# A graph network's node layer: inputs fetched at the batch's own step, three result buffers, the own rows' part computed early; remainders of A and B by a product with minus identity

## The chip, the cores and the metric

The kernel runs on one core of a Trainium2 chip. The metric is device time in microseconds (us), the median over runs of the whole program; lower is better. PE is the matrix engine, DVE the vector engine, ACT the engine for functions and copies, POOL the general-purpose engine that also issues the indirect transfers, SP the engine that issues most other transfers. "Clock" is the share of PE's full clock that was granted in a stretch of time.

## The reference

One layer of a graph network on 12500 nodes with 64 features and 212500 edges (each of 100000 pairs in both directions, and 12500 loops), sorted by destination; the hidden width is 128. All is float32.

```python
h = jnp.maximum(_layernorm(x, axis=-1), 0.0)
edge_in = jnp.concatenate([h[row], h[col], dist], axis=1)   # row = src, col = dst, dist = edge weight
e = jax.nn.silu(edge_in @ eW1 + eb1)
e = jax.nn.silu(e @ eW2 + eb2)
agg = jax.ops.segment_sum(e, row, num_segments=h.shape[0])
node_in = jnp.concatenate([h, agg], axis=1)
out = x + jax.nn.silu(node_in @ nW1 + nb1) @ nW2 + nb2
```

## The kernel before

**Tiles.** The nodes are in NB = 100 buckets of L = 125, and four buckets (G) make a batch: 25 batches. The first edge layer is split by its inputs, A = h @ eW1[:64] for the source and B = h @ eW1[64:128] for the destination, both made once per node. PE's fast format (fp32r, which `halves` marks) holds fewer bits than float32, so each table row stores a value as its fp32r part and the remainder, and later products add the two. The tables `ta` (A) and `tb` (B) are in DRAM; `tb00` and `tb0` hold B's first 512 and 2048 rows, for the first blocks of edges.

**First stage, A and B.** `normed` normalizes 12 buckets of x at a time. `products` (L751) then takes one batch of four: `turned` (L717) transposes four buckets on PE into `ht` (L721) and ACT copies them to `hr` (L725); `product` (L238) multiplies by eW1's half, two PSUM tiles `ab` with two matmuls each (L246); ACT rounds them to fp32r (L250); after a `yield`, DVE subtracts that part from PSUM to leave the remainder (L253). It does so for A, stores `hr` into the DRAM tensor `hd` (L759) and the rows into `ta`, then for B and `tb`. `first_rows` (L728) does the same for B's first rows. `turns(todo, 3)` runs up to three such generators in turn, and each `yield` is a place where other work is put between.

**Sends.** The edges lie in 208 blocks of 1024. For a block, `count` ranks its edges within their buckets (one-hot comparisons on DVE, running counts through PE into the PSUM tile `misc`, L439 and L463), and `send` fetches B's rows by a selection product on PE (`qp`, L493), copies them to `qs` on ACT (L505, L508; eight buffers), and POOL scatters them by indirect transfers, 128 edges each (L515), to the DRAM queue `q`, at bucket and rank. `send_all` walks over the blocks in pieces: half a block of the send beside a step of the next block's count. During the first 8 blocks and then up to the first level's mark (L905 to L923), two to four yields of the first stage are taken per piece. `counted` (L461) also checks the running counts against the limits that the layout assumes and collects violations in `bad`.

**Levels and batches.** A bucket's queue is read in 14 LEVELS of one or two tiles of 128 edges for each bucket; each level goes through all 25 batches. A batch's `qt` (edges out of `q`, `fetch`, L566, four buffers, so four batches ahead) and `a` (rows of A, `fetch_a`, L581, three ahead) come by SP. A step treats four tiles: `s_one` (L644, one-hot of the place in the bucket, compared with `spots` in PSUM), `s_turn` (its transpose `lr`, L601), `s_pt` (L609: transposed `qt` plus A's rows, then Silu on ACT), `s_bias` and `s_p2` (second layer, L661), `s_seg` (L675, the sum per node into the PSUM tile `seg`), `s_add` (L686, into `aggT` in SBUF). `turn` (L693) lists these in the order in which they are written for successive steps, with `None` where pieces of sends, of the first stage, or of the node layer go in.

**Node layer.** In the last level each batch, once its sums are complete, gets `nodes` (L305). PE forms `z` in two PSUM tiles, the sums' part `w1g` (L312) and the own rows' part `w1n` (L315), 250 columns each; ACT applies Silu; a second product gives `o` (L321); DVE adds x (plus the bias) to `os` (L324); SP sends `os` to the output (L326). Its inputs come through `nodes_in` (L296): `xr`, two loads by SP (L126) and the bias added by POOL, and `hrn`, the load of `hd`. `nodes_in` is called in `fetch` (L579), so four batches ahead, with six buffers (pool `nd_in`); results have two (pool `nd`).

**Order.** The order of PE, DVE, ACT and SP is the order in which the program writes the instructions (`manual_schedule`, L340). How many pieces of sends are put at each `None` follows from fixed marks and planned times (`marks`, L931; `PLAN_...`, L64). PSUM has four rotating buffers for `ab`, `ht`, `qp`, `lr`, `pt`, `z` and `o` (pool `mm`), two for `p2`, one each for `misc` and `seg`. At the very end DVE and PE reduce `bad` to a flag (L976 to L984), which is loaded (L985) and, if it is set, starts a general path (L986) that the given inputs do not take.

Of the kernel before, what the change touches and what calls it, by code (L numbers as in the profile page):

```python
# [28 lines left out]
F32 = mybir.dt.float32  # L29
# [10 lines left out]
P = 128  # L40
# [39 lines left out]
def tile_gnn(ctx: ExitStack, tc: tile.TileContext, x, src, dst, ew, eW1, eb1, eW2, eb2, nW1, nb1, nW2, nb2, out):  # L80
# [112 lines left out]
    nodes_i = const.tile([P, L], I32, name="nodes_i")  # L193
# [3 lines left out]
    diff = const.tile([P, P], I32, name="diff")  # L197
# [3 lines left out]
    for a in range(2):  # L201
        half = slice(a * D, (a + 1) * D)
        nc.gpsimd.dma_start(w1[half, :, :], eW1[: 2 * D, :].rearrange("(s k) f -> k s f", s=2))
    same = const.tile([P, 1], F32, name="same")
# [32 lines left out]

    def product(s, hr, ps, tag, to):  # L238

        abs_ = []  # L240
        for a in range(2):

            half = slice(a * D, (a + 1) * D)
            ab = ps.tile([P, G // 2, H], F32, name="ab", tag=tag)
            for i in range(G // 2):
                nc.tensor.matmul(ab[:, i], hr[half, i, :], w1[half, s, :], start=True, stop=True)  # L246
            abs_.append(ab)
# [3 lines left out]
        yield  # L251
        for a in range(2):
            nc.vector.tensor_tensor(to[:, a, 1], abs_[a], to[:, a, 0], op=OP.subtract)  # L253

    hd = dram.tile([P, NB // 2, P], F32, name="hd")
# [40 lines left out]
    def nodes_in(B, sb):  # L296
# [4 lines left out]
        hr = sb.tile([P, G // 2, P], F32, name="hrn")  # L301
        nc.sync.dma_start(hr, hd[:, b // 2 : b // 2 + G // 2, :])
        return xr, hr

    def nodes(B, xr, hr, ps, sb, tag):  # L305

        b = B * G

        zs = sb.tile([P, 2, G // 2, L], F32, name="zs")
        z = [ps.tile([P, G // 2, L], F32, name="z", tag=tag) for _ in range(2)]  # L310
        for a in range(2):
            nc.tensor.matmul(z[a], w1g, aggT[:, b + a : b + G : 2, :], start=True, stop=False)  # L312
        for a in range(2):
            half = slice(a * D, (a + 1) * D)
            nc.tensor.matmul(z[a], w1n[half, :], hr[half, :, :L], start=False, stop=True)  # L315
        for a in range(2):
            nc.scalar.activation(zs[:, a], z[a], AF.Silu, bias=nb1c)
        yield
        o = ps.tile([L, G, D], F32, name="o", tag=tag)
        for t in range(G):  # L320
            nc.tensor.matmul(o[:, t, :], zs[:, t % 2, t // 2, :], w2n, start=True, stop=True)  # L321
        yield
        os_ = sb.tile([L, G, D], F32, name="os")
        nc.vector.tensor_tensor(os_, o, xr, op=OP.add)  # L324
        yield
# [9 lines left out]
    with ExitStack() as work:  # L335
# [8 lines left out]
        misc = sgp.tile([P, 2 * NB + L], F32, name="misc")  # L344
        upto, numbers, spots = misc[:, :NB], misc[:, NB : 2 * NB], misc[:, 2 * NB :]
        nc.tensor.matmul(upto, before, none, start=True, stop=True)
# [131 lines left out]

        def send(s):
# [56 lines left out]
        def send_all(s0, s1):  # L536

            for s in range(s0, s1):
# [19 lines left out]
        batch, st = {}, {}  # L558
# [3 lines left out]
        def fetch(i):  # L562
# [15 lines left out]
            if c == len(LEVELS) - 1:  # L578
                node_in[B] = nodes_in(B, ndp[0])  # L579
# [29 lines left out]
        def s_pt(k):  # L609
# [23 lines left out]
            c, B, n, g = steps[k]  # L633
            if g == n - 1:
                fetch(c * (NB // G) + B + NQ)
                fetch_a(c * (NB // G) + B + NA)

        def s_one(k):
# [7 lines left out]
                spots[:, None, None, :].to_broadcast(wide),  # L646
# [30 lines left out]
        def s_add(k):  # L677
# [9 lines left out]
            if c == len(LEVELS) - 1:  # L687
                tails.append(nodes(B, *node_in.pop(B), mm, ndp[1], "mm"))
# [39 lines left out]
        def first_rows(g):  # L728
# [4 lines left out]
            yield from product(1, hr, mm, "mm", got)  # L733
# [17 lines left out]
        def products(b0, g, xs):  # L751
# [12 lines left out]
            yield from product(1, hr, mm, "mm", got)  # L764
# [355 lines left out]
```

## Time and profile before

| | before |
|---|---|
| median of 3 runs | 2370.76 us (2369.83 to 2371.57) |
| the profiled execution's own time | 2367.31 us |
| its span in the profile | 2365.5 us |
| mean granted clock | 0.892 |
| PE busy | 2028.7 us, 86% |
| DVE busy | 1814.7 us, 77% |
| ACT busy | 1333.0 us, 56% |
| POOL busy | 1655.9 us, 70% |
| moved by DMA | 572.83 MB, mean 242 GB/s |

The profile is of one execution. The page cuts the span into 40 slices of 59 us with a digit for the busy share of each engine in tenths. Rows that begin with a line number group all instructions of that line, engine and operation: count, busy time, mean ns of one, then the idle time of the engine just before them and what ended most of it. Timelines give start and duration in us and, in brackets, the idle time before an instruction and its releaser. PEld is PE's loading of weights, which overlaps its matmuls. POOL's gap of 0.30 between two scatters is not counted as busy, so its 70% is its share without those gaps.

### The profile page before, as it was taken

Reading aid. Unit: us, or ns where it says so; the run is one execution under the profiler, and the core shown is the slowest. Engines: PE = TensorE matmul, PEld = TensorE weight load, DVE = VectorE, ACT = ScalarE, POOL = GpSimd, SP = SyncE. Lnnn points to the kernel's source line nnn. Section 1 sums busy time; section 2 is a strip of 40 time slices with the busy share of each in tenths; the row PEclk is TensorE's granted clock in tenths of the full one; section 3 lists DMA queues with packets and bytes.
Section 4 is the critical chain, followed back from the end, with each engine's and each line's share of the span. In section 5 each row is a group of like instructions: output and inputs, shape, how many; then the busy total and the mean of one; then the engine's idle time right before and its main releaser. Section 6 shows DMA issues by size and latency. Waiting matters only on the chain.

```text
span 2365.5 us, 47589 instructions
## 1 busy us (share of the span) xinstructions
PE 2028.7 (86%) x16818; PEld 1902.7 (80%) x16818; DVE 1814.7 (77%) x2865; ACT 1333.0 (56%) x2966; POOL 1655.9 (70%) x1724
## 2 busy tenths in 40 slices
PE   4667798952599779969995999999999999989997
PEld 2455697942499669959995999999999999989885
DVE  8899788885488868886886888888888888875221
ACT  3334464631277547737773777666666666656542
POOL 5777777777777777777777777777777777776110
PEclk9655597965699879979996999999999999999998
DMA  5566797964488647867884888888888888878662
GB/s 161 188 235 231 268 298 248 324 225 133 155 297 263 224 170 250 264 197 255 288 286 143 284 280 265 268 276 271 285 267 291 274 275 277 272 244 277 196 196 85
DMA packets 239835, 572.83 MB, mean 242 GB/s; under 512 B 46756, under 2 KB 99072, under 8 KB 239177
## 3 DMA queue, kind: packets, MB, share of 16 engines
q1 hardware_dynamic: 155283, 390.76, 51.5%
q0 software_dynamic: 54112, 124.65, 14.4%
q10 hardware_dynamic: 30196, 54.31, 7.3%
q8 instruction: 136, 2.23, 0.4%
q14 instruction: 108, 0.88, 0.1%
HBM read 356.61 MB, written 212.87 MB: 241 GB/s over the span
## 4 chain that ended last, share of the span: by engine, by line
PE 58%; DMA 12%; DVE 11%; POOL 6%; issue 4%; ACT 2%; SPq 2%; POOLq 0%; DVEq 0%; ACTq 0%
PE seg L675 15%; PE p L661 14%; PE pt L622 10%; DMA q<-qs,to 8%; PE pt L615 6%; POOL q L515 6%; PE qp L493 6%; PE lr L601 4%; DMA out_dram<-os 3%; DVE each L434 1%; DVE oh L426 1%; PE bc L379 1%; DVE rank L453 1%; DVE terms L451 1%; DVE pick L415 1%
## 5 line engine op out<-in xcount | busy, mean ns | idle before, releaser
L515 POOL DMA_INDIRECT q<-qs,to x1661 | 1616.1, 973 | 526.5 <-issue 396.9
L631 ACT ACTIVATE e<-pt 128x512 f32<-128x512 f32 x450 | 268.7, 597 | 496.2 <-PE pt L622 495.2
L675 PE MATMUL seg<-one,e 128*128 128x125 f32 x3600 | 502.3, 283 | 2.0 <-DVE aggT L686 1.7
L661 PE MATMUL p<-w,e 128*128 128x128 f32 x3600 | 498.6, 282 | 0.0
L661 PEld LDWEIGHTS p<-w,e 128*128 128x128 f32 x3600 | 449.9, 195 | 9.9 <-issue 9.2
L675 PEld LDWEIGHTS seg<-one,e 128*128 128x128 f32 x3600 | 444.2, 193 | 9.4 <-issue 4.9
L622 PE MATMUL pt<-oneT,a 125*128 125x128 f32 (+1 forms) x2800 | 423.0, 289 | 14.4 <-DMA a<-ta 8.5
L493 PEld LDWEIGHTS qp<-win,pick 128*128 128x128 f32 x1664 | 268.5, 224 | 202.6 <-ACT qs L505 121.6
L493 PE MATMUL qp<-win,pick 128*128 128x256 f32 x1664 | 347.7, 340 | 93.5 <-ACT qs L505 60.6
L505 ACT COPY qs<-qp 128x512 f32<-128x512 f32 x418 | 245.1, 587 | 323.9 <-DMA q<-qs,to 222.9
L622 PEld LDWEIGHTS pt<-oneT,a 125*128 125x128 f32 x2800 | 356.8, 194 | 18.3 <-issue 9.7
L644 DVE TENSOR_TENSOR one<-misc,qt 128x500 f32<-128x500 f32 x450 | 302.4, 672 | 78.1 <-PE seg L675 42.1
L686 DVE TENSOR_TENSOR aggT<-aggT,seg 128x500 f32<-128x500 f32 x325 | 218.4, 672 | 185.9 <-PE seg L675 182.2
L434 DVE TENSOR_REDUCE each<-oh 128x100 bf16<-128x800 bf16 x208 | 321.0, 1543 | 7.2
L615 PE MATMUL pt<-ident,qt 128*128 128x128 f32 x1800 | 276.3, 277 | 10.4 <-ACT qs L505 10.1
L606 ACT CAST oneT<-lr 125x512 fp32r<-125x512 f32 x450 | 265.5, 590 | 13.2 <-PE lr L601 13.2
L665 ACT ACTIVATE e<-p 128x512 f32<-128x512 f32 x450 | 268.7, 597 | 6.1 <-PE p L661 6.1
L655 ACT COPY p<-b2f 128x512 f32<-128x512 f32 x450 | 267.2, 594 | 0.0
L451 DVE TENSOR_TENSOR terms<-oh,misc 128x800 f32<-128x800 bf16 x208 | 203.6, 979 | 38.2 <-PE misc L439 38.2
L615 PEld LDWEIGHTS pt<-ident,qt 128*128 128x128 f32 x1800 | 215.3, 144 | 19.7 <-ACT qs L505 11.0
L453 DVE TENSOR_REDUCE rank<-terms 128x8 f32<-128x864 f32 x208 | 219.0, 1053 | 7.2
L426 DVE TENSOR_TENSOR oh<-misc,bkt 128x800 bf16<-128x800 f32 (+1 forms) x209 | 203.8, 975 | 2.4 <-ACT bkt L831 2.4
(153 smaller groups left out, 1653.4 us busy)
## 6 DMA issues: line engine op xcount, KB each, us to landing
a<-ta SPq DMA_DIRECT2D x350, 512.0 KB
qt<-q SPq DMA_DIRECT2D x250, 288.0 KB
qt<-q SPq DMA_DIRECT2D x100, 576.0 KB
q<-zeros ACTq DMA_DIRECT2D x25, 1080.0 KB
q<-qs,to POOLq DMA_INDIRECT x1661
win<-tb SPq DMA_DIRECT2D x208, 120.0 KB
tb<-got SPq DMA_DIRECT2D x30, 512.0 KB
q<-zeros ACTq DMA_DIRECT2D x20, 720.0 KB
```

What stands on the lines that cost most here:

```text
L434: nc.vector.tensor_reduce(each, oh.rearrange("p t b -> p b t"), AX.X, OP.add)
L493: nc.tensor.matmul(qp[:, t % 2, :k], halves(pick[:, t * P : (t + 1) * P]), halves(win[:, :k, v]), start=v == 0, stop=v == 1,)
L515: ins = nc.gpsimd.indirect_dma_start(out=q[:], out_offset=bass.IndirectOffsetOnAxis(ap=to[:k, j : j + 1], axis=0), in_=qs[:k, t % 2, a, :] ...
L606: nc.scalar.copy(halves(oneT), st[k].pop("lr"))
L615: nc.tensor.matmul(pt[:, t, :], qt[:, j, :H], ident, is_transpose=True, start=t == 0, stop=False, skip_group_check=True)
L622: nc.tensor.matmul(pt[:, cols, :], halves(a[:L, b, i * H : (i + 1) * H]), halves(oneT[:, cols, :]), start=False, stop=i == 1, skip_group_c ...
L631: nc.scalar.activation(e1, pt, AF.Silu)
L644: nc.vector.tensor_tensor(one.rearrange("p (b j) l -> p b j l", j=n), spots[:, None, None, :].to_broadcast(wide), loc[:, tiles[0][1] : til ...
L655: nc.scalar.copy(p2, b2f)
L661: nc.tensor.matmul(p2[:, t, :], e1[:, t, :], w2, start=False, stop=t == G - 1, skip_group_check=True)
L665: nc.scalar.activation(e2, p2, AF.Silu)
L675: nc.tensor.matmul(item[2][:, b, :], e2[:, t, :], one[:, t, :], start=j < G, stop=j >= G * (n - 1))
```

## The change

- `product` does not yield any more. After ACT's two copies of the fp32r part, PE multiplies that part by `less` (minus identity, made once by DVE) and adds the result into the same PSUM tiles, which then hold the remainder; ACT copies that, where DVE subtracted.
- `products` computes the own rows' part of the node layer, `w1n` times `hr`, for its batch: two matmuls, two ACT copies into `zos`, and a store into the DRAM tensor `own` (250 KB for a batch; it replaces `hd` with 128 KB).
- `nodes` starts from that sum: DVE copies the batch's `zo` into PSUM (`bank`, which lies in `misc`), one matmul over all 500 columns adds the sums' part, and one ACT Silu follows. The copy for the next batch is written behind the `os` of this one. Since `misc` is overwritten, the last level's `s_one` compares with `nodes1` in SBUF.
- `nodes_in` is called in `s_pt` of the batch's own step; the pool of inputs has five buffers instead of six, that of results three instead of two.
- The last level's `fetch` calls are held back until three batches before that level, and then catch up; the last mark of the sends moves with them.
- The last turns of the loop have an order of their own (`ending`).
- The flag is made right behind the last `counted`, in the midst of the last level, by `flagged`; the call that loads it is still written behind the loop, while in the order of the built program SP has the load right behind `flagged`.

```diff
+    less = const.tile([P, P], F32, name="less")
+    nc.vector.tensor_scalar(halves(less), ident, -1.0, None, op0=OP.mult)
...
-                nc.tensor.matmul(ab[:, i], hr[half, i, :], w1[half, s, :], start=True, stop=True)
+                nc.tensor.matmul(
+                    ab[:, i], hr[half, i, :], w1[half, s, :], start=i == 0, stop=False, skip_group_check=True
+                )
...
             nc.scalar.copy(halves(to[:, a, 0]), abs_[a])
-        yield
         for a in range(2):
-            nc.vector.tensor_tensor(to[:, a, 1], abs_[a], to[:, a, 0], op=OP.subtract)
-
-    hd = dram.tile([P, NB // 2, P], F32, name="hd")
+            nc.tensor.matmul(
+                abs_[a], halves(less), halves(to[:, a, 0]), start=False, stop=True, skip_group_check=True
+            )
+        for a in range(2):
+            nc.scalar.copy(halves(to[:, a, 1]), abs_[a])
+
+    own = dram.tile([P, NB // G, G * L], F32, name="own")
...
-        hr = sb.tile([P, G // 2, P], F32, name="hrn")
-        nc.sync.dma_start(hr, hd[:, b // 2 : b // 2 + G // 2, :])
-        return xr, hr
-
-    def nodes(B, xr, hr, ps, sb, tag):
+        zo = sb.tile([P, G * L], F32, name="zo")
+        nc.sync.dma_start(zo, own[:, B, :])
+        return xr, zo
+
+    def nodes(B, xr, zo, ps, sb, tag, bank=None, then=()):
...
+        if bank is not None:
+            nc.tensor.matmul(bank, w1g, sums, start=False, stop=True, skip_group_check=True)
+            nc.scalar.activation(zsv, bank, AF.Silu, bias=nb1c)
...
         nc.vector.tensor_tensor(os_, o, xr, op=OP.add)
+        for more in then:
+            nc.vector.tensor_copy(bank, more())
...
+        bank = misc[:, : G * L]
...
+        def flagged():
+
+            s = wk.tile([P, 1], F32, name="s")
+            nc.vector.tensor_tensor(s, bad[:, 0:1], bad[:, 1:2], op=OP.add)
+            turned_ = mm.tile([1, P], F32, name="turned", tag="mm")
+            nc.tensor.transpose(turned_, s, ident)
+            m = wk.tile([1, 1], F32, name="m")
+            nc.vector.tensor_reduce(m, turned_, AX.X, OP.max)
+            nc.vector.tensor_copy(flag_i, m)
...
                         counted(s)
+                        flagged()
...
+            if c == len(LEVELS) - 1:
+                node_in[B] = nodes_in(B, ndp[0])
             if g == n - 1:
-                fetch(c * (NB // G) + B + NQ)
+                i = c * (NB // G) + B
+                while len(fetched) <= i + NQ and (len(fetched) < final or i + 3 >= final):
+                    fetched.append(0)
+                    fetch(len(fetched) - 1)
                 fetch_a(c * (NB // G) + B + NA)
...
-            yield from product(0, hr, mm, "mm", rows_a)
-            nc.sync.dma_start(hd[:, b // 2 : (b + G) // 2, :], hr)
-            yield
+            product(0, hr, mm, "mm", rows_a)
+            zos = fp1.tile([P, G * L], F32, name=f"zos{b // G % 2}")
+            zo = [mm.tile([P, G // 2, L], F32, name="zo", tag="mm") for _ in range(2)]
+            for a in range(2):
+                half = slice(a * D, (a + 1) * D)
+                nc.tensor.matmul(zo[a], w1n[half, :], hr[half, :, :L], start=True, stop=True)
+            for a in range(2):
+                nc.scalar.copy(zos.rearrange("p (i a l) -> p i a l", a=2, l=L)[:, :, a], zo[a])
+            yield
+            nc.sync.dma_start(own[:, b // G, :], zos)
...
-            start = w * (NB // G) - NQ
+            start = w * (NB // G) - (NQ if w < len(LEVELS) - 1 else 3)
...
+        ending = [(s_add, -2), (s_seg, -1), None, None, (s_add, -1), None, None]
+        for k in range(first, len(steps) + 1):
+            for s in turn if k < len(steps) else ending:
...
-                            for name, bufs in (("nd_in", NQ + 2), ("nd", 2)):
+                            for name, bufs in (("nd_in", NQ + 1), ("nd", 3)):
```

More of the change, by code (lines that the diff above doesn't have):

```diff
@@ L343, in tile_gnn @@
         )
[L344 to L346 removed]
+        misc = sgp.tile([P, G * P], F32, name="misc")
+        upto, numbers, spots = misc[:, :NB], misc[:, NB : 2 * NB], misc[:, 2 * NB : 2 * NB + L]
+        bank = misc[:, : G * L]
+        nc.tensor.matmul(misc, before, none[:, 0:1].to_broadcast([P, G * P]), start=True, stop=True)
         nc.vector.tensor_scalar(numbers, nodes1[:, :NB], -1.0, None, op0=OP.add)
@@ L732, in first_rows @@
             got = fp.tile([P, G, 2, H], F32, name="got", tag="rows")
-            yield from product(1, hr, mm, "mm", got)
+            product(1, hr, mm, "mm", got)
             yield
@@ L763, in products @@
             got = fp.tile([P, G, 2, H], F32, name="got", tag="rows")
-            yield from product(1, hr, mm, "mm", got)
+            product(1, hr, mm, "mm", got)
             yield
@@ L941, in tile_gnn @@
         at = 0
-        for k in range(first, len(steps) + 2):
-            for s in turn:
+        ending = [(s_add, -2), (s_seg, -1), None, None, (s_add, -1), None, None]
+        for k in range(first, len(steps) + 1):
+            for s in turn if k < len(steps) else ending:
                 if s is None:
```

48 lines of the change are left out of this document (21 added, 27 removed).

## The prediction

> **What bounds the kernel now.** I read the page's slices first, then stretches of the span, then POOL's timeline, the chain of waits, and PE and ACT instruction by instruction where the change acts. From the page:
>
> ```profile
> POOL 5777777777777777777777777777777777776110
> PEclk9655597965699879979996999999999999999998
> L515 POOL DMA_INDIRECT q<-qs,to x1661 | 1616.1, 973 | 526.5 <-issue 396.9
> ```
>
> POOL's scatter is equally busy in every slice, though PE's share and clock swing. Four stretches (time; then busy us and count for PE, PEld, DVE, ACT, POOL; granted clock, DMA share, GB/s):
>
> ```profile
> 59.00:177.00 118.00, 77.57 (x354) 58.19 (x355) 106.95 (x188) 44.02 (x126) 85.14 (x85) 0.57 0.60 212
> 1600.00:1800.00 200.00, 197.32 (x1823) 194.00 (x1822) 176.43 (x271) 132.62 (x291) 152.13 (x158) 1.00 0.86 277
> 2093.00:2200.00 107.00, 107.00 (x986) 106.16 (x986) 65.22 (x109) 67.80 (x143) 66.22 (x70) 0.98 0.89 293
> 2200.00:2353.00 153.00, 144.57 (x1121) 123.46 (x1119) 37.17 (x71) 68.88 (x138) 13.98 (x20) 1.00 0.53 158
> ```
>
> 158 scatters in 200 us are 1.27 us each, and 1661 of them are 2110 us: POOL is the bound up to its last scatter. Its timeline shows where it wasn't fed (in brackets the idle time before; 0.30 is normal):
>
> ```profile
> 42.16 1.91 POOL L515 DMA_INDIRECT q<-qs,to  x1 [10.50 <-ACT qs L508]
> ...
> 68.18 0.97 POOL L515 DMA_INDIRECT q<-qs,to  x1 [1.79 <-ACT qs L508]
> 92.30 0.96 POOL L515 DMA_INDIRECT q<-qs,to  x1 [2.98 <-ACT qs L508]
> ...
> 126.13 0.96 POOL L515 DMA_INDIRECT q<-qs,to  x1 [2.73 <-ACT got L250]
> ...
> 2173.32 0.97 POOL L515 DMA_INDIRECT q<-qs,to  x1 [0.30 <-issue]
> ```
>
> These three gaps lose 1.5 + 2.7 + 2.4 = 6.6 us over normal. So the span has three parts: while A and B are made, whatever starves POOL is paid in full, because POOL never idles again; then POOL paces; from about 2093 PE is busy all of 107 us, and after 2200 the node layer rides on each batch. There the chain of waits goes round this loop (start, us):
>
> ```profile
> 2306.90 0.43 DVE os L324
> 2307.35 0.32 SPq L126
> ...
> 2309.09 0.43 SPq L126
> 2309.56 3.47 DMA out_dram<-os
> 2313.16 0.43 DVE os L324
> ```
>
> The sum `os` of one batch frees the buffer for a later `xr`; SP loads that and more, only then sends an older result, and the next `os` waits until that has landed, since results have two buffers: 6.26 us a turn. Without that wait a turn is 5.90 us of PE, from one `z` to the next, 0.62 of it the two own-row products of L315:
>
> ```profile
> 2200.85 0.90 PE z L312 x4
> 2201.75 0.62 PE z L315 x4
> ...
> 2206.75 0.90 PE z L312 x4
> ...
> 2333.60 0.90 PE z L312 x4
> ...
> 2353.00 0.44 DVE os L324
> ...
> 2354.27 0.14 DVE flag_i L984
> ```
>
> **Node layer, part by part.** The inputs of a batch are now loaded in its own step, with five buffers that are free by then, and a result has three: both links of the loop are gone. L315 leaves the step; one product over 500 columns replaces two over 250, at the same 0.90 by column count. PE's turn becomes 5.90 - 0.62 = 5.28. What could hold it above that: DVE gains a copy of 128x500 into the bank, between `os` and the sum into `aggT`. By order, `o` ends 1.19 before the turn's end (0.24 and 0.95 for `lr` and `seg`), `os` takes 0.43 and the copy about 0.67 (the page's 128x500 tensor operations), so it ends with `seg`; the sum into `aggT` follows, 0.67, and `z` is due 1.28 after the turn's start: some 0.4 us to spare. Traffic: 288 KB of `qt`, 512 of `a`, 125 each of `xr` and result, 250 of the saved sum (128 before) are 1300 KB in 5.28 us, 246 GB/s, less than the 293 of the third stretch. On SP the three loads now stand ahead of the turn's `qt` and `a` loads, which have two turns of lead. For 21 turns, from the first `z` to the one at 2333.60: 132.75 before, 21 x 5.28 = 110.9 after, **-21.9**. Bounds: if copy or transfers hold the turn at 5.90, -8.9; nothing goes under 5.28.
>
> From 2333.60 to the end of `os` are 19.8 us. After, by order: `z` and what follows 3.73, then 0.85 for the sum into `aggT`, then 13.2 for the chain through `seg`, `z`, `o` and `os` of the last three batches, one turn fewer but with the last bank copy behind `os`: 17.8, **-2.0** (0 to -3). The flag made after the last `os` ends at 2354.41, 0.97 later than `os`: **-0.9** (0 to -2).
>
> **The flag's new place** costs PE. These rows are PE and DVE around the last count:
>
> ```profile
> 2146.18 0.22 PE L463 MATMUL misc<-each,since 128*128 128x100 bf16 x1
> 2146.43 0.25 DVE L472 TENSOR_TENSOR u<-misc,zone 1x100 f32<-1x100 f32 x1 [1.24 <-PE misc L463]
> 2148.17 0.25 DVE L477 SCALAR_TENSOR_TENSOR misc<-zone,misc 128x100 f32<-128x100 f32 x1
> ```
>
> The new transpose stands right behind L463 on PE and waits for all of DVE's checks and the sum `s`, until about 2148.6; `p2` and the steps behind it wait too, in the stretch where PE has no idle time: **+2.5** (0.2 to 3.5). SP's load of the flag waits for the same, and the `qt` load behind it has two turns.
>
> **A and B: where the sign is decided.** DVE loses 108 subtractions, PE gains 108 products with minus identity and 50 for own rows, ACT 158 copies. A product has no pause in it now, so the 25 groups fall into fewer sends: by order, 50 products, 25 transposes and 25 own-row pairs in 29 half blocks (four scatters, 5.1 us of POOL each, 147 in all), where they filled some 40. The rows, PE and ACT at half clock:
>
> ```profile
> 47.60 1.23 PE L246 MATMUL ab<-w,hr 64*128 64x128 f32 x8 [0.46 <-ACT hr L725]
> 48.76 1.22 PE L493 MATMUL qp<-win,pick 128*128 128x256 f32 x4
> 49.97 0.65 PE L721 MATMUL ht<-ident,x 128*128 128x128 f32 x2
> ```
>
> ```profile
> 47.17 0.37 ACT L725 COPY hr<-ht 128x256 f32<-128x256 f32 x1 [0.34 <-PE ht L721]
> 48.85 0.65 ACT L250 CAST got<-ab 128x256 fp32r<-128x256 f32 x2 [1.31 <-PE ab L246]
> ```
>
> ```profile
> 111.24 1.01 PE L493 MATMUL qp<-win,pick 128*128 128x256 f32 x3 [3.99 <-DVE rows_a L253]
> ```
>
> The last row speaks for the change: PE stood 4 us because a subtraction held a PSUM buffer behind other DVE work. Against it: the minus products wait for ACT's first copies, and all behind them on PE waits too, the next send's `qp` first. A product takes PE 1.23, then a 0.45 gap (copy 0.37, handover 0.08), then two minus products at `qp`'s 0.305: 2.29. The own-row pair is twice L315's 0.62, 1.24. A group: 2 x 2.29 + 1.24 + 0.65 = 6.47, and 0.46 for `hr`; the sends' `qp`, lists and counts some 1.77 a half block. Together 25 x 6.93 + 29 x 1.77 = 225 us at half clock, against POOL's 147; at full clock, with the gaps unshrunk, 25 x (2 x 1.38 + 0.62 + 0.33 + 0.46) + 29 x 0.89 = 130. So each us that PE stays at half clock costs POOL 1 - 147/225 = 0.35 us, and none at full clock. ACT's 135 us fit into 147; DVE, 91% busy in the first stretch, has room now. The scatters' loss of 6.6 goes; the first comes about 1.2 later, as two more products and copies stand before the edge weights' split on ACT. The term is 0.35 t - 5.4, t being the time at half clock: -5.4 to +73. When does the clock rise?
>
> ```profile
> 165.61:169.02 3.41, 3.41 (x21) 2.90 (x19) 2.09 (x4) 0.88 (x3) 2.50 (x4) 0.53 0.52 184
> 169.02:172.43 3.41, 0.13 (x1) 0.00 (x0) 2.97 (x5) 0.30 (x1) 2.80 (x3) 0.97 0.68 237
> 186.09:189.50 3.41, 3.41 (x17) 2.72 (x17) 2.83 (x7) 1.48 (x5) 2.80 (x3) 0.50 1.00 365
> 486.46:489.87 3.41, 2.37 (x22) 2.15 (x20) 3.34 (x4) 2.75 (x8) 2.73 (x3) 1.00 0.93 293
> 489.87:493.29 3.42, 1.61 (x10) 1.26 (x10) 3.32 (x7) 1.62 (x5) 2.51 (x4) 0.97 1.01 346
> 493.29:496.70 3.41, 0.59 (x3) 0.24 (x2) 3.36 (x5) 0.00 (x0) 2.50 (x3) 0.50 1.00 338
> ```
>
> A window of 3.4 us full of PE work raised it once and once not; 69% busy kept it, 47% lost it. In the new stage PE is some 85% busy at half clock, and gap-free runs of 4.8 us (minus products, own rows, a send, the next product: 0.61 + 1.24 + 1.22 + 0.5 + 1.23) come about ten times in the 225 us, every 22; with every second one raising the clock, the first success falls near 45 us. At full clock the stage is some 74% busy, enough to keep it. I take t = 45, nearer the lower end: **+10.3** (0.35 x 45 - 5.4).
>
> The Trainium skill, "TensorE: Matmul & The Clock Gate", section "A second HAM failure mode: psum-queue depth-cycling", tells of a PE that pauses briefly between groups while cycling through PSUM banks and whose clock then swings between half and full; by it t would be some half of the stage, and the time that of the first rival below.
>
> **Sum.** -21.9 - 2.0 - 0.9 + 2.5 + 10.3 = -12.0. The profiled execution took 2367.31 (span 2365.5); the median of the runs is 2370.76, 3.45 more, which I keep: **2359 us**. Larger saved sums (3 MB more to write) hide under a DMA share of 0.60.
>
> **Rivals.** First, slower: PE keeps half clock through the products, its waits for ACT breaking each window. Above t = 78 all gain is gone (0.35 t - 5.4 = 22.3), above 91 it can be told as slower; at half the stage, t = 113, the term is 34 and the time 2383; throughout, 2421. For it: PE never held full clock in 59 to 177 (0.57 granted). Against: there PE waited for DVE, which it won't. Second, the change doesn't do in the last level what it says: the bank copy or a load takes the place of the wait and the turn stays at 5.90, 13.0 more: 2372. For it: one bank, and only 0.4 us to spare. Third, POOL is never starved and the term is -5.4: 2343.
>
> **Chances.** Forecast 0.47, first rival 0.30, second 0.13, third 0.10. What this measurement can tell from no change is about 0.2%, 4.7 us. Faster: forecast and third, less 0.02 at the forecast's edge, 0.55. Within: that 0.02, 0.10 of the second and 0.02 of the first, 0.14. Slower: 0.31. The forecast's own range is t from 15 to 70, 2348 to 2367. The range reaches down into the third and up into the first as far as t = 165: 2344 to 2401.
>
> **What would show it.** Last level: `z` to `z` 5.28, no wait of `os` for the result's transfer; wrong if `z` waits for a DVE copy. Flag: one PE wait of 2.5 us near the last count. A and B: granted clock 1.0 in most of the stretch from 100 to 200, PE waiting for ACT some 0.45 at each minus product, last scatter near 2184. A last scatter after 2196 makes the kernel no faster, and then the forecast is wrong in its choice of t.

## The result, and the profile after

The changed kernel is slower: 2394.11 us (median of 5 runs, 2384.1 to 2401.01) against 2370.76 us (5 runs, 2366.01 to 2371.62); the ratio is 1.0102, 95% interval 1.0084 to 1.0120. The whole interval lies above 1, so it is clear of noise, though small. 2359 had been forecast, with a range that ended at 2401 and a chance of 0.31 for slower. From the page of the profile after:

```profile
span 2392.3 us, 47745 instructions
POOL 5556577777777777777777777777777777777210
PEclk9995588895579969996999899999999999999999
L539 POOL DMA_INDIRECT q<-qs,to x1661 | 1615.4, 973 | 580.7 <-issue 392.7
```

POOL's scatter (now L539) takes as long as before, but stood idle before its instructions for 580.7 us, not 526.5, and its row has fives in the first slices where it had sevens: the 54 us are all at the start. Two of the stretches shown before (time; then busy us and count for PE, PEld, DVE, ACT, POOL; granted clock, DMA share, GB/s):

```profile
59.00:177.00 118.00, 94.92 (x427) 72.14 (x430) 72.14 (x114) 64.73 (x194) 63.70 (x64) 1.00 0.59 210
2200.00:2353.00 153.00, 150.45 (x1283) 140.31 (x1283) 65.53 (x118) 86.06 (x159) 37.09 (x44) 1.00 0.82 263
```

In the first, 64 scatters ran where 85 had. DVE has room now (72 us, 107 before), PE does more (95 us, 78 before). POOL's timeline, its longest gaps between 100 and 250, and its last scatter:

```profile
105.23 0.97 POOL L539 DMA_INDIRECT q<-qs,to  x1 [4.82 <-ACT qs L532]
148.58 0.97 POOL L539 DMA_INDIRECT q<-qs,to  x1 [7.99 <-ACT qs L532]
165.18 0.97 POOL L539 DMA_INDIRECT q<-qs,to  x1 [6.71 <-ACT qs L532]
217.32 0.96 POOL L539 DMA_INDIRECT q<-qs,to  x1 [5.58 <-ACT qs L532]
248.21 0.96 POOL L539 DMA_INDIRECT q<-qs,to  x1 [7.41 <-ACT qs L532]
...
2227.56 0.97 POOL L539 DMA_INDIRECT q<-qs,to  x1 [0.30 <-issue]
```

Below, "starving" is the sum over all scatters of the idle time above the normal 0.30, where a gap is longer than 0.5; some 10 us of it is the wait before the first scatter in every kernel. It is 20.0 us before and 74.5 after, and after 300 us there is none. PE's timeline in the last level (the one product of 500 columns is L322) and around the flag's transpose (L498), and DVE's last `os`:

```profile
2203.58 0.27 PE L498 MATMUL turned<-ident,s 128*1 128x128 f32 x1 [2.47 <-DVE s L496]
...
2258.32 1.10 PE L322 MATMUL misc<-aggT,w1g 128*128 128x500 f32 x2
2263.59 1.05 PE L322 MATMUL misc<-aggT,w1g 128*128 128x500 f32 x2
2268.79 1.05 PE L322 MATMUL misc<-aggT,w1g 128*128 128x500 f32 x2
...
2367.70 1.05 PE L322 MATMUL misc<-aggT,w1g 128*128 128x500 f32 x2
```

```profile
2386.02 0.42 DVE L335 TENSOR_TENSOR os<-o,xr 125x256 f32<-125x256 f32 x1 [3.96 <-issue]
```

With the rows of before that stand in the prediction, the two spans divide at the same events. (These rows of before are from the chain of waits, which starts a `z` 0.16 us later than the timeline does; the second and the fourth row are off by that.)

| stretch | before | after | difference | forecast |
|---|---|---|---|---|
| start to the end of the last scatter | 2174.29 | 2228.53 | +54.2 | +10.3 |
| to the first `z` | 26.56 | 29.79 | +3.2 | +2.5 |
| 21 turns to the 22nd `z` | 132.75 | 109.38 | -23.4 | -21.9 |
| to the end of the last `os` | 19.84 | 18.74 | -1.1 | -2.0 |
| to the end of the span | 12.06 | 5.86 | -6.2 | -0.9 |
| span | 2365.5 | 2392.3 | +26.8 | -12.0 |

So the last level gave what was forecast and more, and the first stage took twice that away.

Of the 18 runs below, 14 fell into times when the kernel before itself took 3500 to 3570 us on the same chip ("disturbed" below); of these, times and ratios are not used, only their last level, whose turn is the undisturbed one (5.21 us for the same code), and once a comparison among themselves.

### The profile page after: what moved, and what is told of

Same layout as the page of the kernel before. It is cut to its first block, busy times and chain, and to the rows that moved or that the text cites. A ratio compares the mean times of both kernels' runs of the same rounds, so it can differ in the third digit from the quotient of the medians.

```text
span 2392.3 us, 47745 instructions
## 1 busy us (share of the span) xinstructions
PE 2060.3 (86%) x16827; PEld 1928.7 (81%) x16876; DVE 1797.1 (75%) x2783; ACT 1379.2 (58%) x3099; POOL 1655.7 (69%) x1724
## 3 DMA queue, kind: packets, MB, share of 16 engines
q8 instruction: 136, 2.23, 0.4%
## 5 line engine op out<-in xcount | busy, mean ns | idle before, releaser
L539 POOL DMA_INDIRECT q<-qs,to x1661 | 1615.4, 973 | 580.7 <-issue 392.7
L690 PEld LDWEIGHTS p<-w,e 128*128 128x128 f32 x3600 | 454.0, 196 | 13.1 <-issue 12.3
L673 DVE TENSOR_TENSOR one<-misc,qt 128x500 f32<-128x500 f32 x425 | 285.9, 673 | 78.8 <-PE seg L704 44.1
L630 ACT CAST oneT<-lr 125x512 fp32r<-125x512 f32 x450 | 265.6, 590 | 12.5 <-PE lr L625 12.5
```

What stands on the lines that cost most here:

```text
L539: ins = nc.gpsimd.indirect_dma_start(out=q[:], out_offset=bass.IndirectOffsetOnAxis(ap=to[:k, j : j + 1], axis=0), in_=qs[:k, t % 2, a, :] ...
L630: nc.scalar.copy(halves(oneT), st[k].pop("lr"))
L673: nc.vector.tensor_tensor(one.rearrange("p (b j) l -> p b j l", j=n), (spots if c < len(LEVELS) - 1 else nodes1)[:, None, None, :].to_broa ...
L690: nc.tensor.matmul(p2[:, t, :], e1[:, t, :], w2, start=False, stop=t == G - 1, skip_group_check=True)
```

## The experiments

**What the product costs.** Three runs take the change apart in the first stage. a_old_product and c_yields_kept differ from the changed kernel as the short diffs show; b_minus_only is the kernel before with the change's product, without its yield, and nothing else of the change. Where a product has its yield, the fixed order at the start takes one more turn of `first_rows`.

```diff
# a_old_product: DVE's subtraction again, with its yield
-        for a in range(2):
-            nc.tensor.matmul(abs_[a], halves(less), halves(to[:, a, 0]), start=False, stop=True, skip_group_check=True)
-        for a in range(2):
-            nc.scalar.copy(halves(to[:, a, 1]), abs_[a])
+        yield
+        for a in range(2):
+            nc.vector.tensor_tensor(to[:, a, 1], abs_[a], to[:, a, 0], op=OP.subtract)
# c_yields_kept: the new product, with the old yield in it
         for a in range(2):
             nc.scalar.copy(halves(to[:, a, 0]), abs_[a])
+        yield
         for a in range(2):
             nc.tensor.matmul(abs_[a], halves(less), halves(to[:, a, 0]), start=False, stop=True, skip_group_check=True)
```

> The changed kernel with the old product: remainders by DVE's subtraction, with its yield; all else of the change stays. Theory 1 (the stage of A and B is now a chain on PE and ACT of some 6.9 us per group, whatever the clock, of which the minus products and their waits are 2 x 1.1): the extra starving of POOL (74.5 us in gaps after, 20.0 before) falls to 20 to 30, so the time is some 2340 to 2352. Theory 2 (it is the pacing: four yields per group in place of six put 2.25 groups, not 1.5, ahead of each block's sends): yields are back, so the same, 2338 to 2348. Theory 3 (the own rows' part, 1.21 us of PE and 0.64 of ACT per group, is what starves POOL): starving stays above 45, time 2365 to 2385.

> The kernel before with the new product alone (minus identity, no yield); node layer, own rows and flag as before. Theory 1: 25 groups of 5.7 us and some 33 half blocks of 1.77 against POOL's 5.1 each: starving 30 to 50, time 2380 to 2400. Theory 2: the pacing is that of the change (four yields per group), starving 50 to 75, time 2400 to 2425. Theory 3: no own rows in the stage, starving near 20, time 2366 to 2376.

> The changed kernel with the yield kept inside the product, between ACT's first copies and the minus products, so six yields per group as before and other work between copy and minus product; the same instructions as the change. Theory 1: the waits of PE for ACT are filled, PE work stays: starving 30 to 50, time 2350 to 2370. Theory 2: starving near 20, time 2338 to 2348. Theory 3: starving 45 to 75, time 2365 to 2395.

**Pace or waits.** d3_unsplit_slow has the changed kernel's product, whole, and gives the two lost yields of a group back as empty ones behind the products:

```diff
             for a in range(2):
                 nc.scalar.copy(zos.rearrange("p (i a l) -> p i a l", a=2, l=L)[:, :, a], zo[a])
             yield
+            yield
...
             product(1, hr, mm, "mm", got)
             yield
+            yield
```

> The changed kernel with the number of yields of before, but none inside a product: one empty yield behind each product, so six per group; the same instructions as the change and as c_yields_kept. (Third time: on the first two chips the kernel before itself took 3560 us.) Pacing theory (four yields per group put 2.25 groups ahead of each block's sends): POOL's starving falls from 74.5 us to 20 or less, time 2334 to 2346, even if PE stays slow (four qp products take 1.22 us, as in nearly all of the changed kernel's stage). Clock theory (what helps in c_yields_kept is that other work fills PE's 0.45 us waits for ACT, so that PE gets fast: there half of the groups of four qp take 0.74): the waits are back, PE stays at 1.22, starving 30 to 50, time 2355 to 2375.

The same kernel had run twice before, disturbed:

> The changed kernel with the number of yields of before, but none inside a product: one empty yield behind each product, so six per group; the same instructions as the change and as c_yields_kept. Pacing theory (four yields per group put 2.25 groups ahead of each block's sends): POOL's starving falls to 20 or less, time 2334 to 2346, even if PE stays slow (four qp products take 1.22 us, as in nearly all of the changed kernel's stage). Clock theory (what helps in c_yields_kept is that other work fills PE's 0.45 us waits for ACT, so that PE gets fast: there many groups of four qp take 0.74): the waits are back, PE stays at 1.22, starving 30 to 50, time 2355 to 2375.

> The changed kernel with the number of yields of before, but none inside a product: one empty yield behind each product, so six per group; the same instructions as the change and as c_yields_kept. (Once more, since on the first chip the kernel before itself took 3561 us.) Pacing theory (four yields per group put 2.25 groups ahead of each block's sends): POOL's starving falls to 20 or less, time 2334 to 2346, even if PE stays slow (four qp products take 1.22 us, as in nearly all of the changed kernel's stage). Clock theory (what helps in c_yields_kept is that other work fills PE's 0.45 us waits for ACT, so that PE gets fast: there half of the groups of four qp take 0.74): the waits are back, PE stays at 1.22, starving 30 to 50, time 2355 to 2375.

Measured, with the groups of four `qp` products before 275 us that took under 0.9 us (PE fast) and over (PE slow), and with the scatters that had started when the last product of the stage began, and when that was:

| kernel | yields a group | time | ratio to before, 95% interval | starving | `qp` fast / slow | scatters by the last product |
|---|---|---|---|---|---|---|
| before | 6 | 2370.76 | 1 | 20.0 | 0 / 40 | 168 at 270 us |
| the change | 4 | 2394.11 | 1.0102 (1.0084 to 1.0120) | 74.5 | 1 / 29 | 128 at 272 us |
| b_minus_only | 4 | 2392.38 | 1.0092 (1.0075 to 1.0109) | 43.5 | 2 / 40 | 128 at 242 us |
| a_old_product | 6 | 2351.12 | 0.9922 (0.9905 to 0.9938) | 30.4 | 6 / 33 | 168 at 279 us |
| d3_unsplit_slow | 6 | 2350.91 | 0.9929 (0.9906 to 0.9952) | 24.8 | 11 / 27 | 169 at 280 us |
| c_yields_kept | 6 | 2336.79 | 0.9863 (0.9846 to 0.9879) | 12.3 | 20 / 20 | 170 at 266 us |

The last column shows what a yield does: with four a group 128 scatters stand among the products, with six 168 to 170, whatever PE's speed and work.

c_yields_kept differs from the change by where the yields stand and by nothing else, and is 57 us faster; it beats both kernels. It has all 108 minus products and the own rows' part, and starves less than the kernel before (12.3 against 20.0). With its yield, the new product is better than DVE's subtraction (12.3 against 30.4 in a_old_product), and without it worse (43.5 in b_minus_only against 20.0).

The ranges alone did not decide between the first two theories. a_old_product and b_minus_only came out inside those of theory 1 (a_old_product's starving just above it, its time 3 us above theory 2's), while c_yields_kept, at 2336.79, came out 13 us below theory 1's and 1 below theory 2's. The last column settles it: both have a part. The pace sets how many scatters stand among the products. The work of the products themselves sets how long they take, and at four yields a group that is paid too: b_minus_only, which has no own-row pairs, began its last product 30 us earlier than the change, with the same 128 scatters, and starved 31 us less. The third theory, own rows alone, falls: b_minus_only has none in the stage and starves for 43.5, where that theory said near 20.

d3_unsplit_slow divides the effect: 50 of the 62 us of starving come back with two empty yields a group, while PE's waits for ACT in front of the minus products are still there (28.5 us in all, 25.5 in the change); the other 12.5 come with the split, where these waits are 11.9 us. PE was also fast in more of its groups than in the change, but its products didn't end earlier for it: they took 8 us longer, beside 41 more scatters, which are 52 us of POOL's work at 1.27 each. POOL's timeline in d3_unsplit_slow has these gaps over 0.5 left:

```profile
42.95 1.90 POOL L539 DMA_INDIRECT q<-qs,to  x1 [10.45 <-ACT qs L532]
51.67 0.97 POOL L539 DMA_INDIRECT q<-qs,to  x1 [2.97 <-ACT hr L757]
81.31 0.96 POOL L539 DMA_INDIRECT q<-qs,to  x1 [2.91 <-ACT qs L532]
93.89 0.97 POOL L539 DMA_INDIRECT q<-qs,to  x1 [2.02 <-ACT qs L532]
147.64 0.97 POOL L539 DMA_INDIRECT q<-qs,to  x1 [1.66 <-ACT qs L532]
278.81 0.97 POOL L539 DMA_INDIRECT q<-qs,to  x1 [6.64 <-ACT qs L532]
```

Its time came out some 5 us above what the pacing theory allowed, and its starving 5 above; it stayed under what the clock theory said, by 4 us in time and by 5 in starving. So it lies between the two, in starving and in time alike.

**PE's waits alone.** g4_fillers leaves the change's pace and puts small products of zeros where PE waits for ACT, to leave no pause there:

```diff
+    def fill_pe():
+
+        spare = p2p.tile([P, G, H], F32, name="p2")
+        for _ in range(4):
+            nc.tensor.matmul(spare[:, 0, :NB], before, none, start=True, stop=True)
...
             nc.scalar.copy(halves(to[:, a, 0]), abs_[a])
+        fill_pe()
...
             nc.scalar.copy(hr, ht)
+            fill_pe()
```

> The changed kernel, pace and order untouched, with four small products of zeros (128x100, into a spare PSUM tile) put behind each copy that PE waits for (hr, and ACT's first copies), so that PE has no pause there; they change no result. Clock theory: four qp products fall from 1.22 to 0.74 us in most of the stage, starving from 74.5 to 30 or less, time 2340 to 2360. Pacing theory: PE may get fast or not, but the groups still stand in bursts ahead of the sends; starving stays above 45, time 2365 to 2400.

> The changed kernel, pace and order untouched, with four small products of zeros (128x100, into a spare PSUM tile) put behind each copy that PE waits for (hr, and ACT's first copies), so that PE has no pause there; they change no result. (Once more, as above.) Clock theory: four qp products fall from 1.22 to 0.74 us in most of the stage, starving from 74.5 to 30 or less, time 2340 to 2360. Pacing theory: PE may get fast or not, but the groups still stand in bursts ahead of the sends; starving stays above 45, time 2365 to 2400.

> The changed kernel, pace and order untouched, with four small products of zeros (128x100, into a spare PSUM tile) put behind each copy that PE waits for (hr, and ACT's first copies), so that PE has no pause there; they change no result. Clock theory: four qp products fall from 1.22 to 0.74 us in most of the stage, starving from 74.5 to 40 or less, time 2340 to 2362. Pacing theory (d3 has shown that two empty yields a group take 50 us of starving away): PE may get fast or not, the groups still stand in bursts ahead of the sends; starving stays above 50, time 2365 to 2400.

> The changed kernel, pace and order untouched, with four small products of zeros (128x100, into a spare PSUM tile) put behind each copy that PE waits for (hr, and ACT's first copies), so that PE has no pause there; they change no result. Clock theory: four qp products fall from 1.22 to 0.74 us in most of the stage, starving from 74.5 to 40 or less, time 2340 to 2362. Pacing theory (d3 has shown that two empty yields a group take 50 us of starving away): PE may get fast or not, the groups still stand in bursts ahead of the sends; starving stays above 50, time 2365 to 2400.

All four runs of it (g_fillers to g4_fillers) were disturbed, so what was expected of its time is not answered. Among disturbed runs it can be set against d_unsplit_slow and d2_unsplit_slow, two disturbed runs of the kernel above: with the fillers 6 to 9 of 25 to 27 `qp` groups were fast and POOL starved for 107 to 110 us up to 330; with the empty yields 1 and 4 of 30 and 32 were fast and it starved for 82 and 85. The one with the slower PE starved less, which speaks for the pace. It does not show that PE's speed alone is worth nothing: the fillers are work for PE too, and in g4_fillers PE still stood 36 us in front of the minus products (25.5 in the change), so the pauses were not gone. The number of scatters by the last product was again 128 with four yields a group, and 169 with six. The fourth combination, a split product at four yields a group, wasn't tried. How much of the last 12.5 us between d3_unsplit_slow and c_yields_kept is PE's waits, and how much its clock, stays open.

**The last level.** n3_inputs_early is c_yields_kept with the inputs loaded in `fetch` again, six buffers for them and two for results. o_own_late is c_yields_kept with `hr` saved and the own rows' products in the last level.

```diff
# n3_inputs_early
             batch[c, B] = [qt, None, None]
+            if c == len(LEVELS) - 1:
+                node_in[B] = nodes_in(B, ndp[0])
...
-                            for name, bufs in (("nd_in", NQ + 1), ("nd", 3)):
+                            for name, bufs in (("nd_in", NQ + 2), ("nd", 2)):
# o_own_late
+        z = [ps.tile([P, G // 2, L], F32, name="z", tag=tag) for _ in range(2)]
+        for a in range(2):
+            nc.tensor.matmul(z[a], w1g, aggT[:, b + a : b + G : 2, :], start=True, stop=False)
+        for a in range(2):
+            half = slice(a * D, (a + 1) * D)
+            nc.tensor.matmul(z[a], w1n[half, :], zo[half, :, :L], start=False, stop=True)
```

> c_yields_kept with the node layer's inputs loaded in fetch, four batches ahead, six buffers for inputs and two for results, as before the change; own rows' part still early. If the loop through os, xr's load, the result's transfer and the next os sets the turn, it is about 6.26 us again in place of 5.21: 21 turns give +22, time 2358. Rival: the turn was long because of PE's own-row products, and stays 5.2 to 5.4: time 2337 to 2341.

> c_yields_kept with the node layer's inputs loaded in fetch, four batches ahead, six buffers for inputs and two for results, as before the change; own rows' part still early. (Once more, as above.) If the loop through os, xr's load, the result's transfer and the next os sets the turn, it is about 6.26 us again in place of 5.21: 21 turns give +22, time 2358. Rival: the turn was long because of PE's own-row products, and stays 5.2 to 5.4: time 2337 to 2341.

> c_yields_kept with the node layer's inputs loaded in fetch, four batches ahead, six buffers for inputs and two for results, as before the change; own rows' part still early. If the loop through os, xr's load, the result's transfer and the next os sets the turn, it is about 6.26 us again in place of 5.21: 21 turns give +22, time 2358. Rival: the turn was long because of PE's own-row products, and stays 5.2 to 5.4: time 2337 to 2341.

> c_yields_kept with the own rows' part in the last level again (hr saved and loaded, four products of 250 columns and two Silu per batch, no copy into the bank); inputs at the batch's own step, three result buffers, minus products and flag stay. By the prediction's term the turn is 5.21 + 0.69 = 5.90 us, 21 turns +14.5; the stage of A and B loses 25 x 1.2 us of PE, so starving stays at 12 or falls a little: time 2346 to 2352. Rival: DVE's copy into the bank, now gone, held the turn too, and it grows by less than 0.4: 2337 to 2345.

All were disturbed, but not in the last level (the median turn of n_inputs_early to n3_inputs_early is 6.34, 6.27 and 6.31); their times are not answered. `os` in n3_inputs_early (what DVE's idle time before it was ended by), two of its products of 500 columns, and two `z` of o_own_late:

```profile
L336 DVE TENSOR_TENSOR os<-o,xr x25: 424/425/426, 3404.3 to 3552.1; 125x256 f32<-125x256 f32 x25
its engine sat idle before it (us, times) until:
  DMA out_dram<-os: 57.0, 13
```

```profile
3464.67 1.10 PE L323 MATMUL misc<-aggT,w1g 128*128 128x500 f32 x2 [1.08 <-DVE aggT L716]
3471.02 1.10 PE L323 MATMUL misc<-aggT,w1g 128*128 128x500 f32 x2 [0.93 <-DVE aggT L716]
```

```profile
3456.36 1.06 PE L324 MATMUL z<-aggT,w1g 128*128 128x250 f32 x4
3462.25 1.06 PE L324 MATMUL z<-aggT,w1g 128*128 128x250 f32 x4
```

With early inputs and two result buffers the loop is back: `os` waited 13 times for the result's transfer, and the turn is 6.3 us, although the own rows' part is not in it. With the own rows late and the new buffers it is 5.89. So the two halves of this part do not add: the loop alone holds the turn above 6.2, and taking the own rows out is worth 0.68 only once the loop is gone. Taking out the loop alone is worth 0.37, from 6.26 to 5.89.

**The flag.** f2_flag_end is c_yields_kept with the flag made behind the last batch, as before.

```diff
                         counted(s)
-                        flagged()
...
+        nc.vector.tensor_tensor(s, bad[:, 0:1], bad[:, 1:2], op=OP.add)
+        nc.tensor.transpose(fp, s, ident)
+        m = fl.tile([1, 1], F32, name="m")
+        nc.vector.tensor_reduce(m, fp, AX.X, OP.max)
+        nc.vector.tensor_copy(flag_i, m)
```

> c_yields_kept with the flag made at the very end, as before the change. From the last os to the end of the span 5.9 us become 12.0 as in the kernel before; PE's wait of 2.2 us at the flag's transpose and the slow products behind it go, so last scatter to first z shrinks from 31.9 to about 28.3: together +2.5, time 2339. Rival: the 5.5 us more between last scatter and first z come from the held-back fetches, then that stretch stays near 31 and the time is 2342.

> c_yields_kept with the flag made at the very end, as before the change. (Once more, as above.) From the last os to the end of the span 5.9 us become 12.0 as in the kernel before; PE's wait of 2.2 us at the flag's transpose and the slow products behind it go, so last scatter to first z shrinks from 31.9 to about 28.3: together +2.5, time 2339. Rival: the 5.5 us more between last scatter and first z come from the held-back fetches, then that stretch stays near 31 and the time is 2342.

The chain of waits at the end of f2_flag_end, whose span is 3577.1:

```profile
3564.66 0.44 DVE os L336
3565.10 0.04 issue
3565.14 0.39 PE fp L1021
...
3565.87 0.14 DVE flag_i L1024
```

From the end of the last `os` (3565.10) to the end of the span are 12.0 us, as expected; in c_yields_kept and in the change it is 5.9. The rest, the stretch from last scatter to first `z`, was disturbed in f_flag_end and f2_flag_end. It is 31.9 us in c_yields_kept, 5.4 more than before; PE's wait of 2.23 and the slow products behind it (last section) are seen in its trace, the rest is open. h2_flag_later, which put the flag's sum and transpose one piece later, was meant for the same stretch and did not answer either, in both of its runs:

> c_yields_kept with the flag's sum and transpose one piece later, behind another step's products, instead of right behind the last count. If PE's wait of 2.2 us for DVE and the slow products behind it (some 1.5 us) are a loss on the path, last scatter to first z goes from 31.9 to about 28.2 and the time from 2336.8 to 2333. If that stretch is set by the held-back fetches or by the last rows' landing, nothing changes: 2336 to 2338.

> c_yields_kept with the flag's sum and transpose one piece later, behind another step's products, instead of right behind the last count. If PE's wait of 2.2 us for DVE and the slow products behind it (some 1.5 us) are a loss on the path, last scatter to first z goes from 31.9 to about 28.2 and the time from 2336.8 to 2333. If that stretch is set by the held-back fetches or by the last rows' landing, nothing changes: 2336 to 2338.

## Why the prediction was wrong

**The bound was read rightly.** 54.5 us more of starving moved the last scatter by 54.2: whatever starves POOL while A and B are made is paid in full, as the first part says. Its list of three gaps left one out, of 3.11 us at 51.02 us; the change has it too (4.10 at 52.56), so the sign does not hang on it.

**The node layer was right**, and mis-sized by little: 5.21 us a turn where 5.28 was worked out as the least, no wait of `z` for DVE's copy in the 21 turns, and the last three batches 1.1 us shorter where 2.0 was said; there `z` did wait for that copy, for 1.16 us. The second rival, a turn that stays at 5.90, did not come.

**The flag's end** was mis-sized: -6.2 where -0.9 stood. The step counted only the flag's own instructions behind the last `os`. What follows them, the load of the flag and the branch on it, was also behind them; f2_flag_end prices all of it together, at 12.0 in place of 5.9. The wait on PE was right: 2.47 us in the row of L498 (2.5 forecast, 0.2 to 3.5).

**The step that failed is t = 45**, the time that PE stays at half speed in the stage of A and B. PE's timeline of the change between two sends:

```profile
133.70 1.05 PE L517 MATMUL qp<-win,pick 128*128 128x256 f32 x4
...
137.58 0.86 PE L258 MATMUL ab<-rows_a,less 128*128 128x256 f32 x2 [0.49 <-ACT rows_a L256]
138.37 1.21 PE L795 MATMUL zo<-hr,w1n 64*128 64x250 f32 x4
139.36 1.22 PE L250 MATMUL ab<-w,hr 64*128 64x128 f32 x8
140.93 0.86 PE L258 MATMUL ab<-got,less 128*128 128x256 f32 x2 [0.34 <-ACT got L256]
...
142.67 1.23 PE L250 MATMUL ab<-w,hr 64*128 64x128 f32 x8 [0.46 <-ACT hr L757]
144.39 0.86 PE L258 MATMUL ab<-rows_a,less 128*128 128x256 f32 x2 [0.49 <-ACT rows_a L256]
145.18 1.21 PE L795 MATMUL zo<-hr,w1n 64*128 64x250 f32 x4
146.32 1.22 PE L517 MATMUL qp<-win,pick 128*128 128x256 f32 x4
```

Between one send's `qp` and the next stand 12.6 us with three whole products and two own-row pairs, each near the duration that the prediction put down as half speed; a send feeds POOL for 5.1 us. That gives the gap of 7.99 at 148.58. The gap-free run that was to raise the clock within 45 us did so for the first time at 179, more than 130 us after the first scatter, and it did not last: two waits for ACT later, at 185, PE was slow again. "Some 74% busy, enough to keep it" failed as well: in the 3.41 us up to that drop PE was busy for 1.91, 56%, between the 69% and the 47% of the prediction's rows. A second spell, at 267, lasted 3 us. 29 of 30 `qp` groups were slow, so t was nearly the whole of the stage's 225 us, not 45.

This is the first rival, given 0.30, and the time lies between the two that it names (2383 and 2421). For PE slow throughout, the term's formula says 73 where 54.2 was measured, so its rate of 0.35 was mis-sized too: 29 half blocks were counted among the products, and 128 scatters, 32 half blocks, had started by the end. Three half blocks of 5.1 us are most of the difference.

The Trainium skill, "TensorE: Matmul & The Clock Gate", section "A second HAM failure mode: psum-queue depth-cycling", tells of short pauses between groups and a swinging clock. This trace agrees in part, with two short fast spells in 230 us; that the pauses for ACT are what kept PE slow here, as the rival says, no run shows.

**What lay behind that step.** The prediction counted that the groups fall into fewer sends (29 half blocks for some 40), and then took that number as fixed and asked only when the clock rises. The number was the lever. In the change 128 scatters had started when its last product began (272.1 us), in d3_unsplit_slow 169 when its own did (279.9): the same products on a PE that was slow in most groups took 8 us longer, with 41 more scatters beside them. The sum should have priced the removed yield by itself: at half speed the products and 40 half blocks of sends need 25 x 6.93 + 40 x 1.77 = 244 us of PE, against 204 us of scatters at 5.1, 40 us of loss at most; with 29 half blocks it is 78 at most. "A product has no pause in it now" was written as an aside; it was the dearest edit of the change.

**The sign to look for was a bad one.** "Granted clock 1.0 in most of the stretch from 100 to 200" came true, to the letter, in a stage where PE was slow. See the last section.

## What to carry to other kernels

In an order written by hand, a yield is not only a pause, it is a share: removing one changes how much background work stands ahead of every piece of the work that feeds the bound, and the first thing to count after such an edit is how often the bound is fed. Where a matmul waits for a copy of its own result, let other work stand in between. And where two causes hold the same turn, a loop through buffers and an engine's work, one can look worthless while the other stands (the own rows taken out, the turn stayed at 6.3): take both away, or measure each with the other gone.

## What the runs showed of the hardware

**The clock's column can say 1.00 where PE is as slow as at 0.50.** Time of the `qp` products alone in three stretches of the changed kernel (busy us and count; then granted clock):

```profile
45.00:180.00 135.00, 20.50 (x72) 1.00 0.56 200
190.00:260.00 70.00, 11.51 (x40) 0.50 0.57 209
1600.00:1800.00 200.00, 27.67 (x156) 1.00 0.86 276
```

One product takes 0.285, 0.288 and 0.177 us: at "1.00" in the first row it is as slow as at 0.50. PE's timeline there shows one fast spell, and the two windows after it the column's first change:

```profile
178.74 0.66 PE L258 MATMUL ab<-rows_a,less 128*128 128x256 f32 x2 [0.49 <-ACT rows_a L256]
...
180.20 0.74 PE L517 MATMUL qp<-win,pick 128*128 128x256 f32 x4
...
186.72 1.22 PE L517 MATMUL qp<-win,pick 128*128 128x256 f32 x4
```

```profile
182.60:186.00 3.40, 2.39 (x15) 1.65 (x17) 3.14 (x4) 2.25 (x7) 2.63 (x3) 0.86 1.02 336
186.00:189.40 3.40, 3.40 (x17) 2.10 (x15) 0.95 (x2) 1.63 (x6) 1.65 (x3) 0.50 0.86 274
```

The column stands at 1.00 from the start until the first drop, about 185; in this trace it tells PE's speed only from there. The page of before has the same, a 9 in the first slice in which its `qp` took 1.22. The durations of a known product are the surer clock.

**A wait of 2 us can cost more than itself.** In c_yields_kept, PE at the flag's transpose and the step after it, beside the same product a turn later:

```profile
2142.65 0.37 PE L499 MATMUL turned<-ident,s 128*1 128x128 f32 x1 [2.23 <-DVE s L497]
2142.82 1.91 PE L691 MATMUL p<-w,e 128*128 128x128 f32 x8
...
2147.64 1.11 PE L691 MATMUL p<-w,e 128*128 128x128 f32 x8
```

The eight products behind the wait took 1.91 us, not 1.11. The clock's column shows why: it falls to 0.50 at the end of the wait and is back 3.4 us later. Two windows of c_yields_kept, and the one behind the wait in the changed kernel (columns as in the stretches above):

```profile
2139.15:2142.55 3.40, 1.27 (x12) 1.14 (x11) 1.91 (x11) 1.62 (x6) 2.60 (x3) 0.99 0.92 283
2142.55:2145.95 3.40, 3.30 (x18) 3.33 (x19) 1.01 (x3) 1.07 (x2) 2.49 (x4) 0.50 0.37 143
```

```profile
2203.50:2206.90 3.40, 3.32 (x32) 3.35 (x33) 1.94 (x5) 1.08 (x2) 2.79 (x3) 1.00 0.33 128
```

In the changed kernel a wait of 2.47 at the same place left the clock at 1.00, and the products behind it took the normal 1.05. So it does not always happen; what decides it was not found.
